# Four layers on one core: one PSUM ring for all stages, decays scanned in PSUM, inverse deviations as powers on GpSimd, shared factors, and finer steps in a new order

## The chip, the core and the metric

The kernel runs on one core of a Trainium2 chip. Such a core has five engines with a queue each, which run side by side and wait for each other through semaphores: TensorE (PE; its weight loads are listed as PEld), VectorE (DVE), ScalarE (ACT), GpSimd (POOL) and SyncE (SP), which here only issues DMA transfers. SBUF is the working memory of 128 partitions; PSUM has eight banks of 512 float32 values per partition, and TensorE writes only there. The metric is the device time of one execution in microseconds, as the median of three runs. All data are float32.

## The reference

Four sequences of 1024 tokens with 128 channels go through four layers, each added to its input:

```python
x = x + _layernorm(mamba(_layernorm(x)))      # selective scan, 256 channels, 16 states
x = x + _layernorm(moe(_layernorm(x)))        # 8 gelu experts of width 512, top 2 by softmax, one shared expert
x = x + _layernorm(diff_attn(_layernorm(x)))  # 8 heads, two softmax maps each, their difference
x = x + _layernorm(routed(_layernorm(x)))     # causal attention and experts, 8 projections each, sigmoid gates
```

The parts that matter here:

```python
def step(h, inp):                                  # mamba, over time
    dA = jnp.exp(d_t[:, :, None] * A)
    h = dA * h + (d_t * u_t)[:, :, None] * b_t[:, None, :]
    y_t = jnp.einsum('bdn,bn->bd', h, c_t)
...
h = gelu(einsum('th,ehf->tef', x, W1) + b1)        # every expert on every token
y = einsum('tef,efh->teh', h, W2) + b2
out = einsum('teh,te->th', y, combine) + shared(x)
...
attn_w = softmax(dots)                             # H pairs of maps
attn = einsum('bhqk,bhkd->bhqd', attn_w[:, :, 0] - lam * attn_w[:, :, 1], v)
```

## The kernel before

The order of all work is written out by hand: `ORDER` (L201 to L261) is a string of 5,852 letters, and the loop at L1396 runs one step for each. Every engine's queue receives its instructions in that order. So a letter that makes an instruction wait holds up whatever stands behind it in the same queue.

The work falls into three stretches of the string, which the letters `R` and `Z` divide:

- **Mamba and experts.** The four batches are cut into halves of 512 tokens. `F` (L327) runs the front of a half: norm, projections, silu, and delta, the softplus of a projection, as Abs, Relu, Exp and Ln. Then 32 steps follow, one for each of 16 states and two groups of 128 channels: `f` (L495) fetches the rows B and C from DRAM, spread over all partitions; `a` (L501) computes the decay exp(delta A) on ACT into SBUF; `r` (L505) the product du B on POOL; `s` (L509) scans both on DVE into a PSUM bank and multiplies the result with C; `y` (L522) transposes the product on PE and adds it up over the states in two banks. `B` (L410) takes the half through gate, output projection, two norms and the router; `u`, `g`, `d`, `w` (L542 to L579) are the expert layer (product, gelu, product, weighting on DVE with the sum on POOL); `E` (L482) is the closing norm. PSUM is dealt out in fixed shares: a pool of four banks (L265), one for the expert output (L266), one for the scan (L267) and two named `early` (L101).
- **Differential attention.** At `R` (L1416) those pools are closed and a ring of eight banks is opened. A unit is one head and 128 queries: `P` (L871) computes its two score maps on PE, 1024 columns in two banks each; `M` (L882) the row maxima on DVE; `X` (L886) the exponents with their sums on ACT; `c` (L898) the factor -lambda s0/s1 on DVE; `C` (L904) the difference of the maps, for even heads as two operations on POOL, for odd heads as one on DVE; `T` (L914) eight transposes on PE in two banks, copied to SBUF by ACT; `V` (L930) the products with the values. `p` and `q` (L665, L688) are the projections of the next heads, whose results ACT copies out; `k` and `l` (L737) are norm and output projection of a finished batch.
- **Routed attention and experts.** From `Z` (L1433) on, eight threads (two halves of four batches) run their steps: a digit starts a step's products, a letter of `TAKES` (L200) does the rest of it (L1032 to L1384).

Norms take the variance's square root on ACT (`deviations`, L291; `normed`, L1058; L619, L640, L780, L825, L847, L1096) and its reciprocal on DVE. `Ring` (L60) deals banks out while the program is written: `one` picks the bank that was given back longest ago (and, where it can, the mate of one in use), `two` a pair. The expert weights of the last stretch are loaded at `L`, shortly before the first stretch ends (`later_weights`, L581).

The step in which decay, scan and read-out meet:

```python
self.da[n, j] = m3.tile([P, HALF], F32, name="m_da", bufs=6)
nc.scalar.activation(self.da[n, j], self.delta[:, j, :], AF.Exp, scale=neg_a[:, j, n : n + 1])
...
hb, hh = self.hb[n, j], ps_s.tile([P, HALF], F32, name="m_hh")
nc.vector.tensor_tensor_scan(
    hh, self.da[n, j], hb, 0.0 if self.h == 0 else state[:, j, n : n + 1], ALU.mult, ALU.add
)
```

Of the kernel before, what the change touches and what calls it, by code (L numbers as in the profile page):

```python
# [46 lines left out]
def model_kernel(ctx: ExitStack, tc: tile.TileContext, a: dict, out: bass.AP):  # L47
# [52 lines left out]
    ps_v = tc.alloc_tile_pool(name="d_psv", bufs=1, space=PSUM, reuse_waits="tile")  # L100
    early = ps_v.tile([P, 2, HALF], F32, name="d_early")  # L101
    banks = [early[:, j, :] for j in range(2)]
    ring = Ring(early, 2)
# [7 lines left out]

    vec = load(wa, "vec", [P, 2, NV], a["vec"].rearrange("(h p) v -> p h v", p=P), nc.scalar)
# [4 lines left out]
    for b in range(1, B):  # L117
        nc.sync.dma_start(xs[b], x_d[b])
    gate_w = load(wa, "gate_w", [P, E], a["gate_w"], nc.sync)
    b1 = load(wa, "b1", [P, (E + 1) * NK], a["b1"], nc.sync)  # L120
    b2 = load(wa, "b2", [E + 1, C], a["b2"], nc.sync)
    w1 = wa.tile([P, E + 1, FF], F32, name="w1")
    w2 = wa.tile([P, E + 1, NK, C], F32, name="w2")
    nc.sync.dma_start(w1[:, 0:E, :], a["w1"].rearrange("e c f -> c e f"))
    nc.sync.dma_start(w1[:, E, :], a["sw1"])
    nc.sync.dma_start(w2[:, 0:E, :, :], a["w2"].rearrange("e (k p) c -> p e k c", p=P))
    nc.sync.dma_start(w2[:, E, :, :], a["sw2"].rearrange("(k p) c -> p k c", p=P))
# [3 lines left out]
    eps = const.tile([P, 1], F32, name="eps")  # L131
    nc.vector.memset(eps, LN_EPS)
# [5 lines left out]

    def ln_stats(src, n):

        st = small.tile([P, NB, 6], F32, name="ln_st")
        mv = small.tile([P, NB, 2], F32, name="ln_mv")
        for i in range(n):
            nc.vector.bn_stats(st[:, i, :], src[:, i, :])
            nc.vector.bn_aggr(mv[:, i, :], st[:, i, :])
        sd = small.tile([P, NB], F32, name="ln_sd")
        nc.scalar.activation(sd[:, 0:n], mv[:, 0:n, 1], AF.Sqrt, bias=eps)
        rs = small.tile([P, NB], F32, name="ln_rs")
        nc.vector.reciprocal(rs[:, 0:n], sd[:, 0:n])
        return mv, rs  # L150

    def layernorm(dst, src, n):
        mv, rs = ln_stats(src, n)
        for i in range(n):
            nc.vector.tensor_scalar(
                dst[:, i, :], src[:, i, :], mv[:, i, 0:1], rs[:, i : i + 1], ALU.subtract, ALU.mult
            )

    def add_layernorm(dst, src, n, pool):

        y = pool.tile([P, n, C], F32, name="ln_y")
        layernorm(y, src, n)
        nc.vector.tensor_tensor(dst, dst, y, ALU.add)

    def transpose_blocks(dst, src, n, pool, tag):

        for g in range(0, n, 4):
            ps = pool.tile([P, HALF], F32, name="tr_ps", tag=tag)
            m = min(4, n - g)
            for i in range(m):  # L170
                nc.tensor.transpose(ps[:, i * P : (i + 1) * P], src[:, g + i, :], ident)
            nc.scalar.copy(dst[:, g * P : (g + m) * P], ps[:, 0 : m * P])
# [16 lines left out]
    def normalized(dst, w, n, pool):  # L189
# [10 lines left out]
    TAKES = "GHIJKNOQ"  # L200
    ORDER = (  # L201
        "FFFFFFFFFFFFFFFFFFfFFfaafFrarrasafrfyarasfFafyaafssyyrffrrasassararyafyssaarsyrfsrafsFrFyrrfFFyrFafy"
        "syFaFrsfryyafffrsrsaFasyyyyaassysfyrfsrrarrysrsFayFasyafrraasyssyrFFaFyFsFsrysFraFayFrraraayfFsyfsyy"
        "FyasBBaFsraBaBrsByBsaBrBFrrfsByyBryrsFByBFFryFrBrafasBuryaugBfssFguBurFgsrryFyasayFuyrBgasysasugBuug"
        "ugusgydgyssyadsruyarasaaafgguuwuFrdfryrrygsradgrsasuwgfuydyyysdagfgfsrrayrFuuduywsfyuuasuragdauusags"
        "ygdfFrrggggwyyurgrsrrysyuasfdsyuauygsfgFasasBgBBrguraByawauBayydrdssayusrafggyafrFdawrBsrgdruygBaFfB"
        "urwssfByBuFgsdgBfyyFBsaaBrruararBryBaFaaayffsfsdywuugFrFsgsBfruysussgdrggyysuarauruyarrggryfssgBFyFB"
        "sruryugyaafuudarayfagsuwgasaydsdsudsFfgrwyuugrEayysgaFafyygrsFygudfgrEdywasuuFssuaygyysguBrfuggaEfau"
        "BgsduByauyrsrgudaBgrdwsgrsarrfurdBaaywfaryggFdsyruurBggwdrugBBsyugrfFuuBdgFFrFswsfguBryuudgygufaaFaB"
        "asrFyrsasrBdgwurguusydyafygFfsaysuadggsswygayaaasFFBuFyuFdyguryufgrdsaBuFaFfssarasyBrsrufgrywuyrrrBF"  # L210
        "ssfgBrygFgyrsaBuyagFsEdayfdyrwssyEFgyuEdudygfuuduuwgFFgursadusagugrygawarfsugyfgydfggBsByrusBaduyuBa"
        "aBuawausaugrrgsyrfgagdBdggssugarFuaaaurwsBFfsydygyBsrufgfyrFfsdrgrByBrauysraFFsruyFwsBdgBgayaBfsayru"
        "rsaaBrrrduBuwfrgyFuBggysrFsysFyuguyssdfdryaasFyuuggfgusryggwauByrauasrfFdgaBdaFawaursgfudryuygasfdyy"
        "uusraFdrFarguwgguuygFadsFggrfuusggFFryugdaswsyfyuyurasaFsdgfrgauggyuFarddswsasuyFgrBrBgsBuuaBfrurfag"
        "sgywsBygddaByusfugyrwgyfsarsyauyrFrardrBuassgFyFdFfrByaugsywssFFraydFsBdsyufuyyrBayayaagrBFwBggsufrB"
        "gEfugsdaBdrrfuasraayuEudswggarsBduEgBsyfguuyfrurrygFggaBuBaysdduwuursfyFgguswgddrgfugaasausgyuurguFw"
# [443 lines left out]
    class Batch:  # L660
# [76 lines left out]
        def tail(self):  # L737
# [90 lines left out]
            for i in range(NB):  # L828
# [3 lines left out]
                if i % 2:  # L832
                    yield None
# [715 lines left out]
```

## Time and profile before

| | |
|---|---|
| median of three runs | 2511.61 us (2510.46 to 2514.8) |
| span of the profiled execution, first to last instruction | 2514.4 us |
| instructions | 33745 |
| busy: PE, PEld | 2274.2 us (90%), 1201.7 us (48%) |
| busy: DVE, ACT, POOL | 2123.5 (84%), 1909.2 (76%), 1236.4 us (49%) |
| mean granted TensorE clock | 0.966 of full |
| first decay, first expert product | 39.4 us, 155.0 us |
| last read-out of a scan, first and last score product | 824.7 us, 933.9 us, 1944.2 us |
| ACT table loads started before 934 us, from there to 1954, after | 236, 15, 47 |

The profiled execution's own span is 2.8 us above the median. PE is an engine's row of matmuls, whose ends are modelled: they overlap, so a busy PE is not PE at its peak. A table load is an instruction of 1283 ns that ACT runs before a function of another set than the last one's. The idle time before a group of instructions belongs to its engine, and the releaser is what ended it.

### The profile page before, as it was taken

Reading aid. Unit: us, or ns where it says so; the run is one execution under the profiler, and the core shown is the slowest. Engines: PE = TensorE matmul, PEld = TensorE weight load, DVE = VectorE, ACT = ScalarE, POOL = GpSimd, SP = SyncE. Lnnn points to the kernel's source line nnn. Section 1 sums busy time; section 2 is a strip of 40 time slices with the busy share of each in tenths; the row PEclk is TensorE's granted clock in tenths of the full one; section 3 lists DMA queues with packets and bytes.
Section 4 is the critical chain, followed back from the end, with each engine's and each line's share of the span. In section 5 each row is a group of like instructions: output and inputs, shape, how many; then the busy total and the mean of one; then the engine's idle time right before and its main releaser. Section 6 shows DMA issues by size and latency. Waiting matters only on the chain.

```text
span 2514.4 us, 33745 instructions
## 1 busy us (share of the span) xinstructions
PE 2274.2 (90%) x11462; PEld 1201.7 (48%) x11462; DVE 2123.5 (84%) x4081; ACT 1909.2 (76%) x3049; POOL 1236.4 (49%) x619
## 2 busy tenths in 40 slices
PE   4579899999999988989999999999998899999998
PEld 2345454454545444445455545544554444444443
DVE  4989899998989639998899989998999878777766
ACT  4579999999989648989989898999899434343434
POOL 4958778877768116665555655565556000000000
PEclk7689999999999999999999999999999989999999
DMA  6323333333333330111111111111110000000000
GB/s 188 101 86 109 103 110 93 109 115 97 106 101 108 104 106 1 51 35 54 40 48 29 43 43 43 43 43 43 43 43 1 1 1 5 5 5 5 1 1 17
DMA packets 84015, 143.15 MB, mean 57 GB/s; under 512 B 11633, under 2 KB 27394, under 8 KB 83842
## 3 DMA queue, kind: packets, MB, share of 16 engines
q1 hardware_dynamic: 82722, 140.14, 19.0%
q8 instruction: 90, 1.47, 0.2%
q10 hardware_dynamic: 1120, 0.86, 0.1%
q14 instruction: 83, 0.68, 0.1%
HBM read 121.29 MB, written 19.66 MB: 56 GB/s over the span
## 4 chain that ended last, share of the span: by engine, by line
PE 42%; ACT 11%; DVE 8%; issue 2%; POOL 0%; DVEq 0%; ACTq 0%; POOLq 0%
PE d_ps L878 8%; PE d_ps L938 7%; PE d_ps L1175 7%; PE d_ps L920 6%; ACT d_pt L888 6%; DVE d_m L884 4%; ACT d_wT L925 3%; PE d_ps L1280 2%; PE d_ps L1302 2%; PE d_ps L1325 2%; PE d_ps L1260 1%; PE d_ps L1153 1%; DVE d_pt L910 1%; PE d_ps L1211 1%; PE d_ps L1069 1%
## 5 line engine op out<-in xcount | busy, mean ns | idle before, releaser
L884 DVE TENSOR_REDUCE d_m<-d_ps 128x1 f32<-128x1024 f32 x512 | 610.1, 1217 | 58.2 <-PE d_ps L878 47.5
L888 ACT ACTIVATE d_pt<-d_ps,d_m 128x1024 f32<-128x1024 f32 x512 | 576.4, 1130 | 40.8 <-DVE d_m L884 38.3
L507 POOL TENSOR_TENSOR m_hb<-m_du,m_bt 128x512 f32<-128x512 f32 x256 | 468.7, 1853 | 127.9 <-PE d_early L525 109.5
L907 POOL TENSOR_TENSOR d_pt<-d_pt,d_cf 128x1024 f32<-128x1024 f32 x128 | 277.2, 2165 | 413.3 <-DVE d_cf L902 236.0
L878 PE MATMUL d_ps<-d_k,d_q 32*128 32x512 f32 x2048 | 299.2, 647 | 77.0 <-ACT d_wT L925 43.2
L925 ACT COPY d_wT<-d_ps 128x512 f32<-128x512 f32 x512 | 286.7, 599 | 44.0 <-PE d_ps L920 43.1
L908 POOL TENSOR_TENSOR d_pt<-d_pt,d_pt 128x1024 f32<-128x1024 f32 x128 | 312.5, 2441 | 10.0
L920 PEld LDWEIGHTS d_ps<-ident,d_pt 128*128 128x128 f32 x2048 | 220.5, 141 | 199.2 <-issue 71.8
L545 PE MATMUL l<-f_xnT,w 128*128 128x512 f32 x576 | 284.7, 606 | 17.3 <-ACT f_ht L552 9.7
L920 PE MATMUL d_ps<-ident,d_pt 128*128 128x128 f32 x2048 | 291.0, 281 | 5.7 <-ACT d_pt L888 1.9
L567 PE MATMUL f_yp<-f_ht,w 128*128 128x512 f32 x576 | 277.7, 613 | 6.2 <-ACT f_acc L576 3.9
L938 PE MATMUL d_ps<-d_wT,d_v 128*64 128x256 f32 x2048 | 248.8, 385 | 1.5 <-ACT d_pt L888 1.4
L552 ACT ACTIVATE f_ht<-l,b 128x512 f32<-128x512 f32 x288 | 185.1, 688 | 37.8 <-PE l L545 29.0
L503 ACT ACTIVATE m_da<-m_delta,neg_a 128x512 f32<-128x512 f32 x256 | 171.3, 714 | 51.5 <-DVE m_hh L515 46.6
L525 PEld LDWEIGHTS d_early<-ident,m_hb 128*128 128x128 f32 x1024 | 128.9, 148 | 132.8 <-issue 73.7
L525 PE MATMUL d_early<-ident,m_hb 128*128 128x128 f32 x1024 | 153.1, 287 | 42.1 <-DVE m_hb L520 42.1
L515 DVE TENSOR_TENSOR_SCAN m_hh<-m_da,m_hb 128x512 f32<-128x512 f32 x128 | 175.5, 1371 | 12.9 <-POOL m_hb L507 1.9
L938 PEld LDWEIGHTS d_ps<-d_wT,d_v 128*64 128x64 f32 x2048 | 137.6, 136 | 97.4 <-ACT d_pt L888 15.9
L515 DVE TENSOR_TENSOR_SCAN m_hh<-m_da,m_state,m_hb 128x512 f32<-128x512 f32 x128 | 174.8, 1366 | 10.5 <-DVE m_hb L520 0.5
L520 DVE TENSOR_TENSOR m_hb<-m_hh,m_ct 128x512 f32<-128x512 f32 x256 | 175.9, 687 | 6.5
L579 POOL TENSOR_TENSOR f_acc<-f_acc,f_cb 128x512 f32<-128x512 f32 x64 | 118.5, 1851 | 127.4 <-DVE f_cb L578 110.1
L567 PEld LDWEIGHTS f_yp<-f_ht,w 128*128 128x128 f32 x576 | 107.0, 195 | 134.0 <-issue 117.7
(292 smaller groups left out, 3541.8 us busy)
## 6 DMA issues: line engine op xcount, KB each, us to landing
m_bt<-m_bcd SPq DMA_DIRECT2D x128, 256.0 KB
m_ct<-m_bcd SPq DMA_DIRECT2D x128, 256.0 KB
f_cb<-f_cbd SPq DMA_DIRECT2D x64, 256.0 KB
d_q<-d_qf SPq DMA_DIRECT2D x128, 128.0 KB
d_qf<-d_qks SPq DMA_DIRECT2D x16, 512.0 KB
d_kf<-d_qks SPq DMA_DIRECT2D x16, 512.0 KB
d_k<-d_kf SPq DMA_DIRECT2D x128, 64.0 KB
x<-in_x_dram SPq DMA_DIRECT2D x4, 512.0 KB
```

The lines of the kernel that those rows point to most:

```text
L507: nc.gpsimd.tensor_tensor(self.hb[n, j], self.du[:, j, :], self.bt[n], ALU.mult)
L515: nc.vector.tensor_tensor_scan(hh, self.da[n, j], hb, 0.0 if self.h == 0 else state[:, j, n : n + 1], ALU.mult, ALU.add)
L525: nc.tensor.matmul(banks[j][:, i * P : (i + 1) * P], self.hb[n, j][:, i * P : (i + 1) * P], ident, is_transpose=True, start=n == 0 and i == 0,
L545: nc.tensor.matmul(self.hp[i], w1[:, e, k * P : (k + 1) * P], self.half.fT, start=True, stop=True)
L567: nc.tensor.matmul(self.yp[e][0], w2[:, e, k, :], ht[:, k % 2, :], start=k == 0 and e < E, stop=k == NK - 1)
L878: nc.tensor.matmul(self.sp[s][1][:, c, :], q[g, self.qb * P : (self.qb + 1) * P], k[g, :], start=True, stop=True)
L884: nc.vector.tensor_reduce(self.m[s], self.sp[s][1], AX.XY, ALU.max, negate=True)
L888: nc.scalar.activation(pt.rearrange("p (c k) -> p c k", c=2), self.sp[s][1], AF.Exp, bias=self.m[s], accum_out=self.se[:, s : s + 1],)
L908: nc.gpsimd.tensor_tensor(p, p, p_2, ALU.add)
L920: nc.tensor.transpose(tp[:, i, :], self.pe[0][:, kb * P : (kb + 1) * P], ident)
L925: nc.scalar.copy(wTs[key][:, :, a, qi * P : (qi + 1) * P], tp)
L938: nc.tensor.matmul(op[a * 64 : (a + 1) * 64, :], self.batch.v[hp][:, c * 4 + i, a * 64 : (a + 1) * 64], wTs[self.n // (2 * QG), c][:, i, a ...
```

## The change

- All stages share one ring of eight banks from the start; the four PSUM pools of the first stretch and the ring that `R` opened are gone. Every step that makes a product takes its bank from the ring, and its second half gives it back.
- The decay takes a bank of the ring, and the scan reads it there and writes its result over it. The read-out with C is a step of its own, `m`, which gives the bank back. `hb` has 9 buffers instead of 7, the rows B and C 4 and 6 instead of 3 and 4.
- Every square root for a norm or a length becomes one or two POOL instructions: add epsilon, then the power -0.5 (or 0.5). DVE's reciprocals of deviations go. The sigmoid of the gates becomes an exponential and a reciprocal.
- du, and the product with the gate's silu, move from DVE to POOL.
- The copies of keys and values out of PSUM move from ACT to DVE.
- One factor step serves both heads of a pair and 128 queries, on two columns. Two units of three are combined on POOL and the third on DVE, instead of even heads on POOL and odd heads on DVE. Each lot of exponent tiles has one more.
- The loads of the first stretch are cut into pieces, which letters `D` place in the order (one for each expert; the inputs of the later batches too); the preparation of weights is placed by `W`. The expert weights of the last stretch are loaded at `Z`.
- Steps are cut finer: a step's product and each part that another engine does have letters of their own (`F`/`A`, `B`/`b`, `E`/`e`, `m`, `h` for the fetch of the expert weighting, `v` for the sum on POOL; in the threads, 65 steps instead of 45). The order is a new one, of 6,866 letters.

```diff
-    ps_v = tc.alloc_tile_pool(name="d_psv", bufs=1, space=PSUM, reuse_waits="tile")
-    early = ps_v.tile([P, 2, HALF], F32, name="d_early")
-    banks = [early[:, j, :] for j in range(2)]
-    ring = Ring(early, 2)
+    ps_b = ctx.enter_context(tc.tile_pool(name="ps", bufs=1, space=PSUM, reuse_waits="tile"))
+    ring = Ring(ps_b.tile([P, 8, HALF], F32, name="banks"), 8)
...
-    nc.sync.dma_start(w1[:, 0:E, :], a["w1"].rearrange("e c f -> c e f"))
+    def weights():
...
+        for e in range(E):
+            nc.sync.dma_start(w1[:, e, :], a["w1"][e])
+            nc.sync.dma_start(w2[:, e, :, :], a["w2"][e].rearrange("(k p) c -> p k c", p=P))
+            if e in (3, 7):
+                nc.sync.dma_start(xs[2 + e // 4], x_d[2 + e // 4])
+            yield
...
+    def power(dst, src, k):
+        nc.gpsimd.tensor_tensor(dst, src, powers[:, k : k + 1].to_broadcast(list(dst.shape)), ALU.pow)
+
+    def inverse_sd(dst, var):
+
+        nc.gpsimd.tensor_scalar(dst, var, LN_EPS, 0.0, ALU.add, ALU.add)
+        power(dst, dst, 0)
...
-    ps = ph.enter_context(tc.tile_pool(name="l0_ps", bufs=4, space=PSUM))
-    ps_e = ph.enter_context(tc.tile_pool(name="f_pse", bufs=1, space=PSUM))
-    ps_s = ph.enter_context(tc.tile_pool(name="m_pss", bufs=1, space=PSUM))
...
+            yield None, lambda _: nc.gpsimd.tensor_tensor(du, delta, uc, ALU.mult) and None
...
         def decay(self, n, j):
-            self.da[n, j] = m3.tile([P, HALF], F32, name="m_da", bufs=6)
-            nc.scalar.activation(self.da[n, j], self.delta[:, j, :], AF.Exp, scale=neg_a[:, j, n : n + 1])
+            self.da[n, j] = ring.one()
+            nc.scalar.activation(self.da[n, j][1], self.delta[:, j, :], AF.Exp, scale=neg_a[:, j, n : n + 1])
...
-            state = Half.state
-
-            hb, hh = self.hb[n, j], ps_s.tile([P, HALF], F32, name="m_hh")
+            state, hh = Half.state, self.da[n, j][1]
+
             nc.vector.tensor_tensor_scan(
-                hh, self.da[n, j], hb, 0.0 if self.h == 0 else state[:, j, n : n + 1], ALU.mult, ALU.add
+                hh, hh, self.hb[n, j], 0.0 if self.h == 0 else state[:, j, n : n + 1], ALU.mult, ALU.add
             )
             if self.h == 0:
                 nc.vector.tensor_copy(state[:, j, n : n + 1], hh[:, HALF - 1 : HALF])
-            nc.vector.tensor_tensor(hb, hh, self.ct[n], ALU.mult)
+
+        def read(self, n, j):
+            held, hh = self.da.pop((n, j))
+            nc.vector.tensor_tensor(self.hb[n, j], hh, self.ct[n], ALU.mult)
+            ring.give(held)
...
         def up(self, i):
             e, k = self.order[i // NK], i % NK
-            self.hp[i] = bank()
-            nc.tensor.matmul(self.hp[i], w1[:, e, k * P : (k + 1) * P], self.half.fT, start=True, stop=True)
+            self.hp[i] = ring.one()
+            nc.tensor.matmul(self.hp[i][1], w1[:, e, k * P : (k + 1) * P], self.half.fT, start=True, stop=True)
...
+                        if nm == "q":
+                            nc.scalar.activation(st[:, cols], ps, AF.Copy, scale=HD**-0.5)
+                        else:
+                            nc.vector.tensor_copy(st[:, cols], ps)
...
-        def factor(self):
-
-            self.cf = factors.take()
-            nc.vector.reciprocal(self.cf, self.se[:, 1:2])
-            nc.vector.tensor_scalar(self.cf, self.cf, self.se[:, 0:1], nlam, ALU.mult, ALU.mult)
+        def factor(self, mate):
+
+            cf = self.cf = mate.cf = factors.take()
+            se = self.batch.ses[:, self.qb, self.h : self.h + 2, :]
+            nc.vector.reciprocal(cf, se[:, :, 1])
+            nc.vector.scalar_tensor_tensor(cf, cf, nlam, se[:, :, 0], ALU.mult, ALU.mult)
 
         def combined(self):
-            p, p_2 = self.pe
-            if self.h % 2 == 0:
-                nc.gpsimd.tensor_tensor(p_2, p_2, self.cf.to_broadcast([P, T]), ALU.mult)
+            (p, p_2), a = self.pe, self.h % 2
+            cf = self.cf[:, a : a + 1]
+            if self.n % 3 < 2:
+                nc.gpsimd.tensor_tensor(p_2, p_2, cf.to_broadcast([P, T]), ALU.mult)
                 nc.gpsimd.tensor_tensor(p, p, p_2, ALU.add)
             else:
-                nc.vector.scalar_tensor_tensor(p, p_2, self.cf, p, ALU.mult, ALU.add)
+                nc.vector.scalar_tensor_tensor(p, p_2, cf, p, ALU.mult, ALU.add)
...
-                exps = [Lot(p4.tile([P, T], F32, name=f"d_pt{s}{i}", bufs=1) for i in range(LAG + 2 - 2 * s)) for s in range(2)]
+                exps = [Lot(p4.tile([P, T], F32, name=f"d_pt{s}{i}", bufs=1) for i in range(LAG + 3 - 2 * s)) for s in range(2)]
...
+                ew = {}
+                for nm in ("q_proj", "k_proj", "v_proj", "o_proj", "e_w1", "e_w2"):
+                    ew[nm] = load(once, nm, [P, E, P], a[nm].rearrange("e c h -> c e h"), nc.sync)
```

The new string begins, and crosses into the second and the third stretch, like this:

```python
"F10576342DFBBDDDDDAFAFAWAFFAFAAFAFFAAFAFAWWDffFFAFAFAFAFAFAFAFAFAAFFAAFAFFaAaarrsmrsymyrffffrrrrrsAm"
...
"gudduuddguuhEeEeSuuggguuggwvhwvgddddggugwwvvddhwpqpqvEeEeEpqeRkkPMPMXXMXMSSPMXcCpqPMMMXXPMXXTPXMXcCT"
...
"cCPMXMXMXCcTVPMCCTTTTPXMXMMTXXTTcCTVTVTTTTCVTTlkVlVZlG0kklkG0llkH1G0H1lkklkllkG0H1G0H1G0lkkllG0Gkkll"
```

## The prediction

> **What bounds the kernel now.** I read the page first (engine totals, slices, chain), then busy time by stretch, cut where the stages change, then each stage's waits, then single rows. Columns of the stretches: length, busy time (and instructions) of PE, PEld, DVE, ACT, POOL, granted clock, DMA.
>
> ```profile
> 0.00:155.00 155.00, 79.30 (x268) 46.38 (x268) 111.46 (x209) 72.57 (x97) 99.90 (x59) 0.71 0.45 131
> 155.00:824.00 669.00, 629.35 (x2242) 325.71 (x2242) 608.27 (x983) 628.88 (x790) 524.70 (x279) 0.98 0.36 104
> 824.00:934.00 110.00, 105.16 (x321) 50.89 (x319) 45.32 (x164) 57.42 (x87) 16.52 (x14) 1.00 0.39 111
> 934.00:1954.00 1020.00, 934.93 (x6821) 519.83 (x6822) 936.12 (x1440) 932.08 (x1718) 594.38 (x267) 0.99 0.13 38
> 1954.00:2514.40 560.40, 525.46 (x1820) 258.90 (x1816) 422.38 (x1287) 218.21 (x359) 0.91 (x2) 0.97 0.02 4
> ```
>
> The first expert matmul runs at 155 us, the last scan at 824, the first score product of the second attention at 933.9, its last value product at 1957. From 155 on TensorE is busy 92 to 96% of every stretch, so it is the floor; in the mamba stretch ACT is as full as PE, and in the attention stretch (934 to 1954) DVE and ACT are. PE's idle time is all that an unchanged amount of matmul work lets one win: 76 us before 155, 40 + 5 up to 934, 85 in the attention, 35 in the last stage: 240 in all. The chain of waits agrees: PE 42%, ACT 11%, DVE 8%.
>
> What PE waits for in the attention (engine and line, what ended the wait, us in total, times, longest):
>
> ```profile
> PE d_ps L878 <- ACT d_wT L925: 43.2, 55, 1.2
> PE d_ps L878 <- ACT d_pt L888: 22.8, 33, 3.1
> PE d_ps L878 <- ACT d_v L733: 2.9, 4, 0.8
> ```
>
> 69 of the 85 us end with ACT giving a PSUM bank back. So there ACT's load decides, and each us that leaves ACT's queue is worth nearly a us until PE is full.
>
> Two more views: groups by line (busy, mean ns, idle before), and the tile m_hb (ns minimum/median/maximum).
>
> ```profile
> L552 ACT ACT_TABLE_LOAD x92 | 118.0, 1283 | 1.6
> L503 ACT ACT_TABLE_LOAD x89 | 114.2, 1283 | 1.6
> ```
>
> ```profile
> L507 POOL TENSOR_TENSOR m_hb<-m_du,m_bt x256: 1259/2186/2300, 40.7 to 820.4; 128x512 f32<-128x512 f32 x128
> L515 DVE TENSOR_TENSOR_SCAN m_hh<-m_da,m_hb x128: 1212/1233/3007, 42.0 to 727.4; 128x512 f32<-128x512 f32 x128
> ```
>
> Table loads are a third of ACT's time in the first 934 us, because the order alternates exp and gelu. And POOL's product has two speeds, 1.26 and about 2.19 us.
>
> **Table loads.** A load stands in the trace wherever ACT goes from one of {exp, gelu, silu, sqrt, ln, sigmoid} to another; copies, Abs, Relu, Square and Identity cost none. Counted so, the trace has 236 up to 934, 15 in the attention, 47 after. Walking the new order with the same rule (sqrt and sigmoid are gone, exps and gelus stand in groups) I count 149, 1 and 19. Saved: 87, 14, 28 loads x 1.283 = 112, 18 and 36 us of ACT. In the row the next instruction starts as the load ends (a load at 142.18 for 1.28 us, the decay at 143.47). The Trainium skill, ScalarE: Activation LUTs, What ACT_TABLE_LOAD costs, adds a drain and says about 2.66 us a switch; by it the 129 loads would be 343 us instead of 166. The trace has no room for the drain, so I keep 1.283.
>
> **The scan.** Decays now lie in PSUM, so the scan reads one SBUF operand, not two. Nearest rows for reading and writing PSUM at once: adding the causal mask in PSUM (L1218, 128 columns) 292 ns, and L520, which reads PSUM at 687 ns for 512, against 692 for L1092 from SBUF alone. So the scan itself stays near 1.26 us (ends 1.21, its minimum, and 1.37, the mean it has now). A decay written to PSUM lies between L925 (0.60) and L1083 (0.78), 29 us or 17 us of ACT either way over all 256, which ACT has free; I keep its 0.714. Whether the slow mode of POOL goes is not shown by any row of this pair. Nearest: in the attention L907 takes 1.89 us where DVE only reduces PSUM, and 2.80 where L910 (two SBUF inputs) starts before it. Ends: nothing, or all 256 products at 1.26 (256 x (1.853 - 1.259) = 152 us of POOL) and all scans at 1.26 instead of 1.37 (28 us of DVE). I take the far end, since L910 is the same kind of pair. It lies beside PE, which waited for m_hb only 3.8 us in the mamba stretch; it matters before 155, where DVE and POOL carry the first half.
>
> **Moved in the first stage.** du (8 x 1.63) and the gate product (8 x 1.23) leave DVE: -23 us; on POOL each costs 2.3 to 2.6 like L401: +40. POOL ends near 641 - 152 + 40, plus the powers, with 934 to lie in. Reciprocals go (-5 us of DVE). The prologue: w_o is prepared after the first norm, which takes out DVE's wait for its load (3.3 us, 6.6 to 9.9); du on POOL gives back 1.3. The scans of half 0 ran from 42 to 126 at 2.6 us each, of which the scan's excess over 1.26 and POOL's slow mode are about 0.3: 32 x 0.3 = 10. I take -6 (0 to -12).
>
> **Powers.** 87 Sqrt on ACT (0.2 to 0.3 us) and their reciprocals on DVE (0.17) become 87 powers on POOL, mostly with an addition before. No row shows a power. From below 0.32 us (L781, 128x64 on POOL), from above 4.4 (L400, the longest POOL row); the tiles are 4 to 24 wide, so I take 0.4. POOL is idle in the last stage and free a third of the first, so they are hidden, except once in the prologue and once at the end (2508.8, Sqrt and reciprocal 0.5 us): together +0.6, at the far end +16.
>
> **Attention.** ACT loses 58 key and value copies (x 0.59 = 34) and 18 us of loads: 932 to 880. DVE gains these copies (L949 is 417 ns at 256, so 0.68 at 512: +39); loses half the factors, now one pair for two heads (256 x (152 + 273) to 128 x about 430: -54); and loses combinations: one unit in three instead of one in two (128 to 85, x 1.30: -56). DVE: 936 to 865. POOL combines 171 units instead of 128, at 2.17 + 2.44 = 4.61 us: 590 to 788, in a stage of 975 or so, and there is a tile more for each exponent lot. A factor now waits for both heads, some 3.7 us later (a unit's share of the stage), with the next row maxima behind it on DVE; those tiles cover it; without that cover it would show as PE waiting for d_pt. ACT's 52 us should come back as PE time but for what PE's own floor of 935 stops: -45 (ends +20 and -85).
>
> **First stage.** PE waits in 155 to 824: 40 us idle, of which some 21 ended with ACT and 14 with DVE. ACT loses 112 us, nearly all of them here, of 629. PE stays: -25 up to 934 (ends +10, -45). At 934 the old pools close and the clock granted falls to 0.68 for 16 us while PE is busy 10.6 of them; one ring needs no such border: -6 (0 to -10).
>
> **Last stage.** PE has 35 us of idle; loads on ACT (60 us) were mostly beside it. -8 (ends +15, -35). The expert weights, 3.1 MB, are now asked for at the stage's start, on SP, behind the last readers of the memory they take (1957). At the 111 GB/s of the 824 to 934 stretch each 0.52 MB lands 4.7 us after the one before: q_proj 1964, k 1969, v 1973; their first uses are 1984, 1991, 1998. Covered; uncovered up to 28 us. The first stage's loads become 24 issues instead of 10, at 0.4 us of SP; SP's last old weight issue alone took 10 us, before the first store at 26, so none is on the path.
>
> Sum: -6 - 25 - 6 - 45 - 8 = -90. Span 2514.4 - 90 = 2424; the median of the runs lies 2.8 under the profiled span, so **2422**.
>
> **Rivals.**
> PE nearly full: idle 45 to 10, 85 to 20, 35 to 20, and -12 for prologue and border: -127, **2385**, and 2365 with all ends. For: ACT ends nearly all attention waits. Against: ACT, at 880, still fills 90% of such a stage.
> POOL becomes the attention's pole: with L907 at its 2.80 throughout, 171 x 5.24 = 896, and PE waits for combined maps; the stage stays near 1010: **2457**. For: 2 of 3 units there. Against: POOL sat idle 413 us before L907.
> It doesn't do what it says: what leaves ACT returns as another wait since PE is over 92% anyway; only prologue or border change: **2507**. For: 94% PE in the mamba stretch. Against: the ACT-ended waits.
> Slower, through **one ring**: decays hold banks from ACT's exp until DVE has read the scan, beside two accumulators, the expert output and the gelu inputs. Walking the order, 5.3 of 8 banks are held on average up to 934, all 8 at 170 of 2961 letters, and 124 takes (55 gelu inputs, 41 decays, 14 fronts, 14 expert outputs) get the bank that was given back last, so that they wait for its reader's end. At about 1 us each (a gelu is 0.69, an L520 0.69 plus the hand over) that is +124 instead of -25: **2570**. Behind a decay that waits stand gelus on ACT, and behind these the banks of PE's next expert products. It decides once PE's share between first expert and last scan falls below about 0.85. Against: the old pool of four banks turned as quickly. The Trainium skill, ScalarE: Activation LUTs, Step-by-step: what each stage is for, says that ACT writes PSUM faster than SBUF but that this is only of use where TensorE doesn't need most of PSUM, which speaks against it here. No row of this trace shows ACT writing PSUM, and the page gives no price.
>
> **Chances.** Forecast 0.52, PE nearly full 0.15, POOL 0.13, nothing 0.08, ring 0.12. The range 2365 to 2510 leaves out the ring and a little of the low end. 0.2% of the time is 5 us, about what this measurement can tell from no change; half of "nothing" lies under it: faster 0.84, same 0.03, slower 0.13.
>
> **What would show it.** Right: about 169 table loads; POOL's m_hb rows near 1.26; PE over 95% and ACT near 90% in an attention of 960 to 985 us; the border at 934 without a clock dip. Wrong: m_hb still at two speeds; PE waiting for d_m or d_pt out of POOL; PE's expert products waiting for DVE's reads of the scan; a scan over 1.4 us; powers of several us ahead of PE work.

## The result and the profile after

The new kernel takes 2711.84 us (median of four, 2708.8 to 2714.9) against 2512.91 us before (2510.5 to 2514.8): a ratio of 1.0795, 95% interval 1.0776 to 1.0813. It is 8% slower; forecast were 2422 us and a range of 2365 to 2510. The profiled execution spans 2707.0 us against 2514.4.

The busy time by stretch of the kernel after, cut at the same events as before (first expert matmul, last scan, first score product, last value product). Columns: length, busy time (and instructions) of PE, PEld, DVE, ACT, POOL, granted clock, DMA share, GB/s.

```profile
0.00:150.00 150.00, 90.00 (x286) 49.80 (x287) 110.80 (x210) 66.23 (x93) 87.81 (x73) 0.69 0.46 140
150.00:758.00 608.00, 581.65 (x2141) 303.53 (x2140) 572.14 (x983) 512.62 (x667) 415.29 (x322) 0.99 0.37 114
758.00:907.00 149.00, 145.87 (x396) 68.18 (x398) 43.15 (x126) 65.46 (x94) 32.22 (x27) 0.98 0.19 58
907.00:2107.00 1200.00, 1011.84 (x6854) 557.46 (x6849) 1005.13 (x1199) 898.02 (x1642) 801.10 (x367) 0.95 0.12 35
2107.00:2707.00 600.00, 528.93 (x1795) 255.66 (x1792) 415.19 (x1252) 168.47 (x277) 73.38 (x85) 0.94 0.01 4
```

The first score product comes at 906.7 us instead of 933.9: 27.2 us earlier. From there to the last value product it takes 1200.6 us instead of 1023.3: 177.3 longer. The last stage takes 599.7 instead of 557.2: 42.5 longer. -27.2 + 177.3 + 42.5 = 192.6, the whole difference of the spans. In the attention stretch no engine is full: PE fell from 92% to 84%, DVE from 92% to 84%, ACT from 91% to 75%; GpSimd rose from 58% to 67%. TensorE's idle time grew from 85 to 188 us, and its busy time from 935 to 1012 us for the same products, at a granted clock of 0.95 instead of 0.99: roughly 100 of the 177 us are waiting, the rest is matmuls that take longer.

What ACT and PE wait for there (kernel after, waits in 907 to 2107: engine and line, what ended the wait, us in total, times, longest):

```profile
ACT d_pt L993 <- DVE d_m L989: 145.0, 124, 12.8
PE banks L983 <- ACT d_wT L1033: 56.2, 73, 1.4
PE banks L983 <- ACT d_pt L993: 33.9, 33, 3.9
```

ACT's exponents wait 145 us for VectorE's row maxima. The same wait in the kernel before:

```profile
ACT d_pt L888 <- DVE d_m L884: 38.3, 90, 1.8
```

The maxima themselves take 1.216 us each, as before (1.217). So something ahead of them on VectorE's queue is late. The groups by line show what (L910 is the combine before, the other lines are the kernel after; busy, mean ns of one, idle before):

```profile
L910 DVE SCALAR_TENSOR_TENSOR d_pt<-d_pt,d_cf,d_pt 128x1024 f32<-128x1024 f32 x128 | 166.3, 1299 | 1.9 <-DVE d_cf L902 0.5
L1017 DVE SCALAR_TENSOR_TENSOR d_pt<-d_pt,d_cf,d_pt 128x1024 f32<-128x1024 f32 x85 | 185.3, 2180 | 0.9
L1008 DVE SCALAR_TENSOR_TENSOR d_cf<-d_cf,d_nlam,d_ses 128x2 f32<-128x2 f32 x128 | 53.4, 417 | 4.5
L749 DVE TENSOR_SCALAR d_w<-x,d_mvs,d_rss 128x128 f32<-128x128 f32 x24 | 23.3, 1031 | 1.0 <-PE banks L843 1.0
L922 DVE TENSOR_SCALAR d_w<-d_w,d_mv,d_rs 128x128 f32<-128x128 f32 x24 | 18.1, 814 | 0.0
```

The combine went from 1.299 to 2.180 us: before, 4 of 128 took over 1.5 us, now 58 of 85 do. The norm of a batch ahead of its projections (L749, L676 before) went from 0.343 to 1.031. The timeline says why. Kernel after, start, length, engine, instruction:

```profile
974.63 2.36 POOL L1015 TENSOR_TENSOR d_pt<-d_pt,d_pt 128x1024 f32<-128x1024 f32 x1
975.33 1.67 DVE L1008 SCALAR_TENSOR_TENSOR d_cf<-d_cf,d_nlam,d_ses 128x2 f32<-128x2 f32 x1
...
986.15 2.35 POOL L1015 TENSOR_TENSOR d_pt<-d_pt,d_pt 128x1024 f32<-128x1024 f32 x1
986.40 3.18 DVE L1017 SCALAR_TENSOR_TENSOR d_pt<-d_pt,d_cf,d_pt 128x1024 f32<-128x1024 f32 x1
...
989.50 2.34 DVE L989 TENSOR_REDUCE d_m<-banks 128x1 f32<-128x1024 f32 x2
990.75 1.11 ACT L993 ACTIVATE d_pt<-banks,d_m 128x1024 f32<-128x1024 f32 x1 [0.38 <-DVE d_m L989]
```

L1008 works on two columns and needs 0.22 us where nothing hinders it; here it ends at 977.00, when GpSimd's addition ends (974.63 + 2.36 = 976.99). L1017 ends at 989.58, 1.08 us after GpSimd's addition (988.50), so all but 0.2 us of its own work comes after it. Then follow two maxima, and ACT's exponent has stood waiting. In the kernel before, VectorE's combine met GpSimd's multiplication the other way round:

```profile
1005.87 1.28 DVE L910 SCALAR_TENSOR_TENSOR d_pt<-d_pt,d_cf,d_pt 128x1024 f32<-128x1024 f32 x1
1006.10 2.80 POOL L907 TENSOR_TENSOR d_pt<-d_pt,d_cf 128x1024 f32<-128x1024 f32 x1 [1.16 <-ACT d_qks L704]
```

There VectorE started first, and GpSimd, which has time, paid 0.9 us. Of the 48 overlaps of L910 with L907, VectorE began first in 37. In the kernel after GpSimd's addition began first in 33 of its 62 overlaps with L1017, and VectorE then took 2.61 us. The page "SBUF — State Buffer" of the Trainium skill, section "Who interferes with whom", says that a VectorE instruction with two SBUF inputs contends with a GpSimd instruction that reads SBUF for a shared pair of ports, that this pair is an exclusive lock, and that the order of issue decides who blocks. The times above agree: the second starts when the first ends, and nothing is shared. Two inputs are not needed for a wait of this kind here: L749 and L922, with one tensor in SBUF and two columns of scalars, took 1.031 and 0.814 us, and 0.343 us each where GpSimd combines nothing (no_gpsimd_combine_after below).

Worked out from the means, with the undisturbed ones of that run (1.278, 0.221, 0.343, 0.343 us): 85 x 0.90 = 77, 128 x 0.20 = 25, 24 x 0.69 = 17 (L749) and 24 x 0.47 = 11 (L922, the norm of a finished batch). About 130 of VectorE's 1005 busy us in this stage are standing still; its work is 875.

The second thing is in the chain of waits (kernel after, its longest pieces by line: start, length):

```profile
1200.61 10.55 POOL d_z L156
1577.75 11.53 POOL d_z L156
1872.82 10.54 POOL d_z L156
```

and in the groups:

```profile
L156 POOL TENSOR_TENSOR d_z<-d_z,powers 128x64 f32<-128x64 f32 x4 | 43.1, 10783 | 22.4 <-ACT d_z L858 22.4
L156 POOL TENSOR_TENSOR r_sd<-r_sd,powers 128x4 f32<-128x4 f32 x32 | 35.0, 1094 | 2.7
```

A power costs 1.03 to 1.16 us on 4 columns and 10.8 on 64. The wide one is the root of the sums by which a finished batch's heads are normed; in each of three batches the chain goes through it. The next longest pieces of the chain are the two norms that wait for GpSimd: 4.75 us for four of L922 and 4.68 us for three of L749.

### The profile page after: what moved, and what is told of

Same layout as the page of the kernel before. It is cut to its first block, busy times and chain, and to the rows that moved or that the text cites. A ratio compares the mean times of both kernels' runs of the same rounds, so it can differ in the third digit from the quotient of the medians.

```text
span 2707.0 us, 33484 instructions
## 1 busy us (share of the span) xinstructions
PE 2358.3 (87%) x11462; PEld 1234.6 (46%) x11462; DVE 2146.4 (79%) x3767; ACT 1710.8 (63%) x2770; POOL 1409.8 (52%) x874
## 4 chain that ended last, share of the span: by engine, by line
PE 51%; DVE 25%; ACT 9%; issue 5%; POOL 3%; DMA 0%; DVEq 0%; POOLq 0%; ACTq 0%; SPq 0%
PE banks L983 7%; PE banks L641 6%; DVE d_m L989 6%; PE banks L618 6%; PE banks L1268 5%; PE banks L1046 5%; PE banks L1028 5%; ACT d_pt L993 4%; DVE d_pt L1017 3%; DVE banks L582 2%; ACT d_wT L1033 2%; PE banks L1404 2%; PE banks L598 2%; POOL d_z L156 2%; DVE r_xin L1391 2%
## 5 line engine op out<-in xcount | busy, mean ns | idle before, releaser
L989 DVE TENSOR_REDUCE d_m<-banks 128x1 f32<-128x1024 f32 x512 | 604.9, 1216 | 83.4 <-PE banks L983 69.8
L993 ACT ACTIVATE d_pt<-banks,d_m 128x1024 f32<-128x1024 f32 x512 | 571.6, 1121 | 149.5 <-DVE d_m L989 145.0
L983 PE MATMUL banks<-d_k,d_q 32*128 32x512 f32 x2048 | 341.8, 672 | 123.3 <-ACT d_wT L1033 56.2
L1033 ACT COPY d_wT<-banks 128x512 f32<-128x512 f32 x512 | 281.0, 591 | 111.3 <-PE banks L1028 110.1
L1028 PEld LDWEIGHTS banks<-ident,d_pt 128*128 128x128 f32 x2048 | 230.3, 145 | 237.0 <-issue 89.2
L1028 PE MATMUL banks<-ident,d_pt 128*128 128x128 f32 x2048 | 300.6, 288 | 39.4 <-ACT d_pt L993 24.3
L618 PE MATMUL banks<-f_xnT,w 128*128 128x512 f32 x576 | 279.3, 608 | 9.0 <-ACT m_uc L372 3.9
L641 PE MATMUL banks<-f_ht,w 128*128 128x512 f32 x576 | 267.4, 600 | 0.5 <-DVE m_hb L590 0.5
L1046 PE MATMUL banks<-d_wT,d_v 128*64 128x256 f32 x2048 | 259.5, 395 | 7.3 <-ACT d_pt L993 7.0
L626 ACT ACTIVATE f_ht<-banks,b 128x512 f32<-128x512 f32 x288 | 191.1, 687 | 107.2 <-PE banks L618 91.6
L1017 DVE SCALAR_TENSOR_TENSOR d_pt<-d_pt,d_cf,d_pt 128x1024 f32<-128x1024 f32 x85 | 185.3, 2180 | 0.9
```

The source lines that it names most:

```text
L618: nc.tensor.matmul(self.hp[i][1], w1[:, e, k * P : (k + 1) * P], self.half.fT, start=True, stop=True)
L641: nc.tensor.matmul(self.yp[e][1], w2[:, e, k, :], ht[:, k % 2, :], start=k == 0 and e < E, stop=k == NK - 1)
L983: nc.tensor.matmul(self.sp[s][1][:, c, :], q[g, self.qb * P : (self.qb + 1) * P], k[g, :], start=True, stop=True)
L989: nc.vector.tensor_reduce(self.m[s], self.sp[s][1], AX.XY, ALU.max, negate=True)
L993: nc.scalar.activation(pt.rearrange("p (c k) -> p c k", c=2), self.sp[s][1], AF.Exp, bias=self.m[s], accum_out=self.se[:, s : s + 1],)
L1028: nc.tensor.transpose(tp[:, i, :], self.pe[0][:, kb * P : (kb + 1) * P], ident)
```

## The experiments

All ratios are against runs of the kernel before on the same chip. "Attention" is from the first score product to the last value product, "last" what follows, both from the profiled execution.

| kernel | time, us | ratio (interval) | first product at | attention | last |
|---|---|---|---|---|---|
| before | 2512.9 | 1 | 933.9 | 1023.3 | 557.2 |
| after | 2711.8 | 1.0795 (1.0776-1.0813) | 906.7 | 1200.6 | 599.7 |
| split_undone | 2781.1 | 1.1064 (1.1036-1.1092) | 908.9 | 1263.5 | 597.7 |
| split_done_in_before | 2622.9 | 1.0445 (1.0423-1.0467) | 935.7 | 1132.2 | 556.7 |
| all_ops_undone | 2758.9 | 1.0982 (1.0956-1.1009) | 908.7 | 1252.6 | 590.9 |
| first_stage_alone | 2500.6 | 0.9949 (0.9931-0.9967) | 914.8 | 1024.7 | 560.5 |
| z_root_back | 2673.8 | 1.0643 (1.0607-1.0680) | 904.7 | 1176.8 | 589.3 |
| no_port_wait | 2645.9 | 1.0526 (1.0489-1.0564) | 909.4 | 1141.1 | 597.0 |
| no_port_wait_z_back | 2617.1 | 1.0414 (1.0375-1.0454) | 911.5 | 1119.9 | 588.1 |
| last_roots_back | 2728.7 | 1.0862 (1.0818-1.0906) | 907.4 | 1200.7 | 616.6 |
| border_mended | 2738.7 | 1.0877 (1.0859-1.0895) | 913.1 | 1232.5 | 598.3 |
| three_together | 2637.2 | 1.0476 (1.0460-1.0492) | 907.4 | 1136.5 | 588.6 |
| first_stage_weights_late | 2495.4 | 0.9915 (0.9901-0.9930) | 914.3 | 1027.9 | 553.4 |
| first_and_last_powers | 2503.8 | 0.9948 (0.9933-0.9963) | 909.6 | 1025.4 | 566.9 |
| no_combine_after | 2561.9 | 1.0187 (1.0166-1.0208) | 906.5 | 1060.4 | 593.2 |
| no_combine_before | 2511.5 | 0.9986 (0.9966-1.0006) | 932.4 | 1017.1 | 559.3 |
| no_gpsimd_combine_after | 2560.6 | 1.0177 (1.0155-1.0199) | 910.6 | 1062.8 | 587.2 |
| copies_moved | 2523.0 | 1.0040 (1.0026-1.0053) | 906.5 | 1055.5 | 556.4 |

**The split, undone and done.** In the kernel after, `self.n % 3 < 2` becomes `self.h % 2 == 0`; in the kernel before, the reverse.

> The kernel after with one rule put back: GpSimd combines the even heads (128 units) instead of two units of every three (171), VectorE the odd ones (128 instead of 85). Theory S (the split costs the time: POOL has 171 x 4.4 us = 753 us of combining in an attention stage of 1200 us and slows VectorE's combine from 1.30 to 2.18 us by sharing the SBUF port): the attention stage falls to 1060-1100 us, the time to 2570-2620 us, and VectorE's combine has a mean under 1.6 us. Theory O (the new order itself costs it: at about 1150-1190 us almost no unit is begun, and the engines wait for each other everywhere else): the time stays within 25 us of 2712.

> The kernel before with this rule of the new one alone: GpSimd combines two units of every three. Theory S: attention 1020 -> 1100 us or more, the time 2590 or more. Theory O: little, since before's order leaves GpSimd idle for 413 us; up to 2540, the second of two GpSimd units in a row coming late by some 4 us.

Undoing made it 69 us slower, doing it in before 110 us. The first contradicts both theories. My reading is that an order is written for one split; what the trace shows is that the 128 combines that VectorE then makes still wait at the port (mean 1.829 us, 234 us in all against 185). The second is plain in its size: two units of three on GpSimd lengthen the attention stage by 109 us even in the order of before. Its cause is not the port alone: VectorE's combine takes 1.609 us there (29 of 85 over 1.5 us), and the transposes wait for GpSimd's addition itself. The weight loads' wait for it in the kernel before, then both rows in split_done_in_before, then the kernel after:

```profile
PEld d_ps L920 <- POOL d_pt L908: 10.5, 15, 1.2
PEld d_ps L920 <- POOL d_pt L908: 40.2, 35, 3.1
PE d_ps L920 <- POOL d_pt L908: 20.0, 13, 2.9
PEld banks L1028 <- POOL d_pt L1015: 8.3, 8, 1.6
```

In the kernel after, the matmuls themselves wait 0.6 us in all for GpSimd's combined maps, so there that wait is not what costs the time.

**Three operations back, order kept.** The split as above, and

```diff
-                            nc.vector.tensor_copy(st[:, cols], ps)
+                            nc.scalar.copy(st[:, cols], ps)
...
-                power(z.rearrange("p m a -> p (m a)"), z.rearrange("p m a -> p (m a)"), 1)
+                nc.scalar.activation(z, z, AF.Sqrt)
```

(the value copy likewise).

> The kernel after with its order as it is, and three of its operations of the attention stage put back: the split of the combining (even heads on GpSimd), the copies of keys and values on ScalarE, the root of the tail's 128x64 sums on ScalarE. Theory S (operations): at most 2570 us. Theory O (order): 2650 us or more, ScalarE busy some 35 us more, and the hole at 1150-1190 us still there.

2759 us: far over 2570, but 22 under split_undone. With the split undone in an order made for another, this run cannot tell the operations from the order; the single edits that follow try to.

**The first stage alone.** Classes and order of the attention and the last stage from before, in the kernel after.

> The first stage of the new kernel (one PSUM ring from the start, decays in PSUM, powers on GpSimd, its part of the order) with the attention and the last stage of the one before, their order included. If the first stage's gain of some 27 us (the first score product at 907 instead of 934 us) is its own, the time is 2480-2492 us. If it was borrowed (work only put off into the attention stage), 2505-2515. If the single ring costs the attention stage, over 2530.

2500.6: an 11 us gain, between the two expectations. The product comes at 914.8, but at 909.6 in first_and_last_powers, which has the same first stage: runs with one first stage differ by that much. Neither the one ring nor the PSUM decays cost the attention stage anything (1024.7).

**The wide power, and the wait at the port.** z_root_back is the Sqrt line above by itself. no_port_wait leaves the 85 combines of VectorE out and puts an instruction of about the same length with one SBUF input in their place:

```diff
-                nc.vector.scalar_tensor_tensor(p, p_2, cf, p, ALU.mult, ALU.add)
+                nc.vector.tensor_reduce(p[:, 0:1], p_2, AX.X, ALU.max)
```

> The kernel after with the root of the tail's 128x64 sums put back on ScalarE (Sqrt); nothing else. Theory Z: the GpSimd power takes 10.8 us and stands three times in the chain of the attention stage (10.55, 11.53 and 10.54 us) and once in the last stage, with all engines behind it; the attention stage falls by 25-35 us and the time to 2670-2685. Rival: the engines are late for other reasons at those places and the wait only moves; the time falls by under 12 us.

> The kernel after with VectorE's combine of 85 units (two SBUF inputs) replaced by a maximum over one of the two tiles into a column of the other: as long (about 1.2 us), same order, same waits before and behind it, but one input; the exponentials of these 85 units are not combined. Theory L (VectorE stands still until GpSimd's instruction ends, 2.18 instead of 1.28 us, and the maxima behind it come late): VectorE's new instruction has a mean of 1.2-1.3 us, the attention stage falls by 60-100 us, the time to 2610-2650. Theory P (GpSimd's load and lateness, 171 x 4.4 us, is what counts): the stage falls by under 30 us.

> Both edits of z_root_back and no_port_wait. If the two are separate causes their gains add up (85-135 us, attention 1065-1115 us). If both only uncover the order's own idle places, the sum is under 60 us. If the whole loss of 180 us in the attention stage is these two, the stage is at 1020-1040.

z_root_back: -38 us, 24 of them in the attention, 10 in the last stage. no_port_wait: the new instruction takes 1.208 us, the stage falls by 60. (GpSimd's addition falls with it, from 2.502 to 2.355 us, since nothing of VectorE's combine stands in its way either.) Both: -81 in the attention against 83 for the two apart. So these are two separate causes. 1119.9 us is still 97 over before.

**The last stage's powers.**

```diff
-            inverse_sd(self.sd, self.mv[:, :, 1])
+            nc.scalar.activation(self.sd, self.mv[:, :, 1], AF.Sqrt, bias=eps)
...
             mv, sd = self.mv, self.sd
+            nc.vector.reciprocal(sd, sd)
...
-            yield None, lambda _: power(self.nn, self.nn, 1)
+            yield None, lambda _: nc.scalar.activation(self.nn, self.nn, AF.Sqrt) and None
```

> The kernel after with the 48 powers of the last stage's parts (32 inverse deviations, 16 lengths) back on ScalarE as Sqrt, with VectorE's reciprocal where the deviation is used. Theory H (each power is a hop over GpSimd of 1.3-1.6 us at a place where VectorE and PE wait): the last stage falls from 600 to 570-580 us. Rival O (the last stage is slower by its new order): it stays at 590 us or more, also because some 30 table loads of 1.28 us come back to ScalarE.

The stage became 17 us longer: these narrow powers help in this order, and are not what made the stage slow. The reverse edit in first_stage_alone is first_and_last_powers.

> first_stage_alone with the last stage's 48 roots as powers on GpSimd, in the order of before. last_roots_back lost 17 us in the last stage by taking them away in the order after; theory T (what counts is ScalarE's table loads, some 30 of 1.28 us, at each of which the chain waits): the last stage falls from 560 to 540-550 us, the time to 2480-2492. Rival: the GpSimd hop (about 1.6 us for a deviation) is as long as Sqrt with its load and the reciprocal: within 5 us.

2503.8, last stage 566.9 against 560.5: no gain in that order.

**The border of two batches.** From the product of unit 63 (counted from 0) to that of unit 64 the new order has 94 letters. The stretch of the string there, before and after the edit:

```diff
-PXMXTMMXlVVlklCkXpqpqlcppqqTTpqTppqpqqklCTTTTkVCTTVVlppqqklkkpqllppkkllkkllqqkkllklpqklklkkllk
+PXMXTMMXVVCXcTTTCTTTTVCTTVV
```

(The 14 pairs p, q go singly behind units 49 to 62; the letters k and l, with those that follow up to unit 111, go evenly behind units 67 to 111.)

> The kernel after with 54 letters of its order moved and nothing else: between the products of units 63 and 64 (the border of the first two batches) stand 14 steps of the second batch's front and 19 of the first batch's tail with no unit between them. The front's steps go one each behind units 49 to 62, as the order before had them, the tail's evenly behind units 67 to 111. Theory O (the order leaves units out there: 14.5 units begun in 80 us where 40 are usual, some 45 us): the attention stage falls by 30-50 us, the time to 2660-2685. Rival: the time is set by VectorE's and GpSimd's waits, which only move: under 15 us.

> The edits of border_mended, z_root_back and no_port_wait together (the exponentials of 85 units are not combined). If the three are separate, they add up to 65 + 37 + 30..50 us: the time is 2560-2580, the attention stage 1065-1085 us. What then stands over 1023 us is the rest of the order and of the port. If they overlap, over 2600.

27 us slower instead of 30 to 50 faster, and 20 us slower on top of the two other edits (2637.2 against 2617.1). So this run does not show that the units missing there are lost time: at the places that I chose, the steps cost more. Better places were not tried.

**Weights late.** first_stage_alone with the last stage's weights loaded at letter Z and one more exponential tile of each kind.

> first_stage_alone with two more things of the new kernel: the 3.1 MB of the last stage's weights asked for at the end of the attention stage instead of before its start, and one more tile for the exponentials of each score matrix. If the early load costs the end of the first stage (0.28 of the DMA engines' time there against 0.19), the time is 5-10 us under first_stage_alone (2491-2496 against 2500.6). If the late load comes too late for the last stage (it takes some 25 us at the 130 GB/s that the prologue shows), 5-20 us over it.

2495.4, and the last stage is 553.4: the late load is covered. This is the fastest version found, 0.9915 of before (0.9901 to 0.9930).

**No combining.** Left out in z_root_back, and the same lines in before; then GpSimd's two alone in z_root_back.

```diff
-                nc.gpsimd.tensor_tensor(p_2, p_2, cf.to_broadcast([P, T]), ALU.mult)
-                nc.gpsimd.tensor_tensor(p, p, p_2, ALU.add)
...
-                nc.vector.scalar_tensor_tensor(p, p_2, cf, p, ALU.mult, ALU.add)
```

> z_root_back with the combining of the two exponentials left out on GpSimd and on VectorE alike (the products go on with the first exponential alone): no instruction of GpSimd stands between exponent and turning any more, none holds the port against VectorE. Beside it the same cut in the kernel before. Theory G (the whole loss in the attention stage comes from GpSimd's combining: its port, its lateness): the stage is as long as in no_combine_before within 15 us. Theory O (the order itself is slower, whatever is combined): it stays 40 us or more longer.

> The kernel before with the combining left out in the same way. Its VectorE has 166 us less and its GpSimd nothing to do in the attention stage; PE, busy 935 of 1020 us, then bounds it alone: 960-1000 us, the time 2450-2490.

> z_root_back with GpSimd's part of the combining alone left out; VectorE still combines its 85 units. Between this and z_root_back lies what GpSimd's 171 units cost, port and lateness together: by theory G 100-150 us (the attention stage at 1030-1075), by theory O 60-75 us, what no_port_wait gave, since VectorE's waits at the port are all that goes.

The groups of no_gpsimd_combine_after (the line after the combine's branch has moved up by one):

```profile
L1016 DVE SCALAR_TENSOR_TENSOR d_pt<-d_pt,d_cf,d_pt 128x1024 f32<-128x1024 f32 x85 | 108.6, 1278 | 0.3
L1008 DVE SCALAR_TENSOR_TENSOR d_cf<-d_cf,d_nlam,d_ses 128x2 f32<-128x2 f32 x128 | 28.3, 221 | 4.5
L749 DVE TENSOR_SCALAR d_w<-x,d_mvs,d_rss 128x128 f32<-128x128 f32 x24 | 6.7, 343 | 1.0 <-PE banks L843 1.0
```

All three groups are back at their own durations, and the stage falls from 1176.8 to 1062.8, by 114 us. Leaving out VectorE's part too changes it by 2. In before, leaving out all of the combining, 166 us of VectorE and 590 of GpSimd, gives 6. (Its own expectation, 960 to 1000 us for the stage, missed: it stayed at 1017.1.) So the combining is nearly free in the one kernel, with its split, and costs 116 us in the other with its own. ACT's wait for the maxima in z_root_back:

```profile
ACT d_pt L993 <- DVE d_m L989: 119.0, 121, 12.8
```

and ACT's waits in no_gpsimd_combine_after:

```profile
ACT d_wT L1032 <- PE banks L1027: 90.9, 118, 2.9
ACT d_pt L993 <- DVE d_m L989: 52.1, 85, 12.8
```

52 instead of 119 us behind the maxima. 57 to 60 of the 114 us go with the combine's own contest for the port (no_port_wait); the other waits at the port that go with GpSimd are worth 25 + 17 + 11 us of VectorE, which leaves little for GpSimd's lateness as such, and in z_root_back the matmuls wait 0.7 us in all for GpSimd's maps. That this second half is the port was argued so, and not tried by itself. What remains against before with equal work, 1060.4 - 1017.1 = 43 us, is the order with the small moves in it (shared factors, copies on VectorE). Neither expectation named this: both causes are real, and what goes with GpSimd's combining is 2.7 times the other.

**ScalarE's load.** The copies of keys and values on VectorE, in first_stage_weights_late.

```diff
-                    yield project, lambda ps, st=st, cols=cols, sc=sc: nc.scalar.activation(
-                        st[:, cols], ps, AF.Copy, scale=sc
-                    )
+                    if nm == "q":
+                        yield project, lambda ps, st=st, cols=cols, sc=sc: nc.scalar.activation(
+                            st[:, cols], ps, AF.Copy, scale=sc
+                        )
+                    else:
+                        yield project, lambda ps, st=st, cols=cols: nc.vector.tensor_copy(st[:, cols], ps)
```

(values likewise).

> first_stage_weights_late (2495.4 us) with the copies of keys and values moved from ScalarE to VectorE, as the new kernel has them: 64 copies of about 0.59 us less on ScalarE, of 0.68 us more on VectorE; they read PSUM and need not wait at the port. no_combine_before showed that VectorE's load does not set the attention stage's length. Theory A (the prediction's reading: ScalarE, giving banks back, ends TensorE's waits): the stage falls from 1028 to 995-1015 us, the time to 2465-2485. Rival F (TensorE's own work and its chain through the banks set it, whoever copies): 1022-1035, the time within 6 us of 2495.

28 us slower. ACT's waits, first in first_stage_weights_late:

```profile
ACT d_wT L997 <- PE banks L992: 43.9, 93, 1.6
ACT d_pt L960 <- DVE d_m L956: 41.1, 92, 4.7
```

and in copies_moved:

```profile
ACT d_pt L963 <- DVE d_m L959: 78.9, 128, 12.8
ACT d_wT L1000 <- PE banks L995: 61.4, 118, 2.5
```

ACT has less to do and waits longer for VectorE, which now has the copies beside the maxima on its queue. I take the copies ahead of maxima for the cause; no run tells a copy's own time from what it shifts.

## Why the prediction was wrong

**What bounds it.** "So there ACT's load decides" is the step on which the forecast of the attention stage stands, and it failed. PE's waits did end with ACT, but a wait that ends with ACT's exponent is as long as the maxima make it. ACT lost 34 us in the kernel after (932 to 898; 52 were predicted), and the stage grew; copies_moved lost ACT's copies and got slower. VectorE's load did not decide before either (no_combine_before: 6 us). My reading is that what counts is how soon each maximum follows its product. Nor was "PE's own floor of 935" a fixed one: with the waits and the lower clock the same products took 1012 us.

**Attention, -45 predicted, +177 measured.** The failing step is "loses combinations (128 to 85, x 1.30: -56)". Each took 2.180 us: 185 us instead of 110, and 19 more than before instead of 56 less. The prediction had the row (L907 at 2.80 us where L910 starts before it) and read it as a price that GpSimd pays. It held "POOL: 590 to 788" (801 measured) for harmless because GpSimd had sat idle 413 us; but more GpSimd time that reads SBUF is more time in which VectorE can't start. VectorE's work was right (865 predicted, 875 by the sum above); the 130 us of standing still had no term. The shared factor was to give 54 and gave 35 (109 us before, 20 + 53 after): its new form has two SBUF inputs and waits at the port, which the old form, with a mean of 0.273 us in every run that has it, did not. Of the 177 us, the runs put 24 on the wide power, 110 on combining as it is split here (116 against 6 in before), and 43 on order and small moves.

**Powers, +0.6 predicted.** The failing step is "the tiles are 4 to 24 wide, so I take 0.4". One is 64 wide (the row of the Sqrt that it replaces, L780, had 128x64), and cost 10.8 us on the chain, outside the bounds of 0.32 and 4.4. All in all it is worth 38 us. No power cost as little as 0.4: those of 4 and 8 columns took 1.03 to 1.7 us, the one of 24 took 4.29. In the last stage of this order they were useful even so (17 us).

**First stage, border and prologue.** -37 predicted up to the first score product, -27.2 measured. The mechanism was right. 170 table loads stand in the trace (169 predicted), of 1.283 us each, and ACT's next instruction starts within 0.05 us of the end of 161 of them: no room for the drain that the forecast left out. The scan takes 1.22 to 1.28 us (1.26 predicted), a decay into PSUM 0.683 (0.714), GpSimd's product 1.285 instead of 1.853 (1.26). The groups of the decay's and the gelu's loads after, and then the tile m_hb (ns minimum/median/maximum):

```profile
L571 ACT ACT_TABLE_LOAD x66 | 84.7, 1283 | 1.2
L626 ACT ACT_TABLE_LOAD x60 | 77.0, 1283 | 2.3 <-PE banks L618 1.2
```

```profile
L575 POOL TENSOR_TENSOR m_hb<-m_du,m_bt x256: 1252/1271/2247, 42.0 to 744.2; 128x512 f32<-128x512 f32 x128
L582 DVE TENSOR_TENSOR_SCAN banks<-banks,m_state,m_hb x128: 1258/1282/1292, 122.2 to 757.0; 128x512 f32<-128x512 f32 x128
```

GpSimd's median fell from 2.186 to 1.271 us. I read it as the port again, with the other sign: of the 256 products before, the 170 that began while a scan ran took 2.08 us on average; with one scan operand in PSUM, the 114 that began so took 1.27. In whole executions the first stage is worth 11 us by itself (0.9949 of before) and 22 with the late weights (0.9915). The border gave nothing: in the first 60 us of the attention the granted clock was 0.83 against 0.89 before, PE busy 42.9 against 47.7.

**Last stage, -8 predicted, +42.5 measured.** 10 us are the wide power of the last batch. The late weights are covered, as forecast. The rest, 32 us, is neither the powers nor the weights. PE is busy 24.4 us in the first 50 (45.0 before) and 30.5 in the last 50 (38.8); with the root back it is 33.2 and 30.3. I take this for the order of the steps at both ends, but no run isolates it.

**The rivals.** "POOL becomes the attention's pole" had the right engine and the wrong mechanism: it never filled the stage (67%), and matmuls waited 0.6 us for its maps; it blocked VectorE. "One ring" had the right sign; but PE held 96% from first expert to last scan, far over its 0.85, and first_stage_alone clears it. No case joined GpSimd's added work to VectorE's instructions, so the slower side got 0.13.

## What to carry to other kernels

Count GpSimd's SBUF-reading instructions and VectorE's two-input ones, and here its norms from SBUF to SBUF too, as users of one resource, and look at who starts first: work moved to an idle GpSimd can be paid on VectorE's queue if GpSimd gets there first. An engine that ends most waits need not be the one whose load decides; leave work out of it once, or out of its neighbours, before building a change on it. Price an operation that the trace does not show by its widest tile, and look whether that one stands in a chain.

## What the runs showed of the hardware

A power on GpSimd goes by columns: 1.03 us for 4, 1.66 for 8, 2.90 for 16, 4.29 for 24, 10.78 for 64, some 0.16 us for each. An instruction of 0.22 us on two columns can wait 2 us for the port, while the reciprocal on the same columns just ahead of it (0.158 us) never does (0.169 at most). And more idle time of TensorE came with a lower granted clock and longer matmuls: in the attention stage it idled 85 us at 0.99 (before), 128 at 0.96 (no_port_wait_z_back), 188 at 0.95 (after) and 225 at 0.92 (split_undone). The same 6862 matmuls were busy 1010.3 us at 0.96 (z_root_back) and 963.9 us at 0.99 (no_gpsimd_combine_after), so 46 of those 114 us are busy time, not idle time.
